# A second table in rank order, stored by SP, its row places carried by the first table; ranks computed ahead

## The chip, the cores and the metric

The kernel runs on one core of a Trainium2 chip. The metric is device time in microseconds (us), the median of several executions. Engines are named as in the profile: PE (TensorE, matmul), PEld (its weight load), DVE (VectorE), ACT (ScalarE), POOL (GpSimd), SP (SyncE, which here only issues DMAs).

## The reference, cut to what matters

A graph network of two layers over 6250 nodes and 100000 edges (sorted by destination), 16 node types, 32 edge types, 8 heads of 16 features, then a linear layer and a norm:

```python
k, q, v = (typed_linear(x, ntype, W).reshape(n, H, HS) for W in (Wk, Wq, Wv))
kT = jnp.einsum('nhd,htdo->nhto', k, Watt)      # for each node and edge type
vT = jnp.einsum('nhd,htdo->nhto', v, Wmsg)
kw = kT[src, :, etype]
m  = vT[src, :, etype]
a  = jnp.einsum('ehd,ehd->eh', kw, q[dst]) * pri[:, etype].T / SQRT_D
att = edge_softmax(a, dst, n)
hag = jax.ops.segment_sum((m * att[:, :, None]).reshape(-1, H * HS), dst, num_segments=n)
h = jax.nn.silu(typed_linear(hag, ntype, Wa))
# h is mixed with x by a gate of the node type, normalised, and is the next layer's x
```

After two layers: `x = layernorm(x + (h @ ff_w + ff_b))`.

## The kernel before, in words

**Tables.** For each layer the kernel writes a table into DRAM: a row for each node and edge type, 256 floats (128 of kT, 128 of vT). A tile `st` holds 128 nodes by 16 edge types by 256, 2 MB; a block of 128 nodes makes two of them (TG = 2). `table_block` (L287) fills one by eight groups of matmuls (L299) that ACT copies out of PSUM (L306), or DVE where `share` says so (L304); then `store` issues its DMA. An edge reads one row, number `src * 32 + etype`, kept in `ell`.

**Preparation and first table (L311 to L1030).** Nodes are sorted by type for the typed linear layers (`place`, `inv`, L371 to L431). `degrees` (L513) counts the edges of each destination: 64 passes over all edges on DVE (L537), four to a group, and for each group one-hot rows (L548 to L557) whose matmuls (L531) add the counts to the nodes. `rank_order` (L644) turns degrees and node types into a rank for each node, so that a block of 128 nodes has nearly equal degrees; rank is complete at L807. Its second half (L808 to L864) brings start, degree and type of each node into rank order, and then POOL gathers edge lists (`ell`, L869) and features (`xr`, L881) by rank. All of this is a generator (`ranking`) that the loop over first-table blocks (L1014 to L1030) advances a step at a time, so ranking and first table run side by side. The first table's rows are stored by `put0` (L1001): an indirect DMA of POOL, as nodes are in order of type there. `fetch` (L943) gathers x blocks for it with POOL.

**Layers (arm, L1034; edges, L1103).** For each of 50 blocks of 128 destinations, POOL gathers one table row per partition and edge slot (L1274), 867 gathers a layer, into `kvr`, a ring of 50 slots. DVE multiplies the rows with q (L1286), reduces (L1290), and `finished` (L1154) does softmax and weighted sums, a step at a time between the chunks of the next block. Three or four blocks make a superblock, of which there are 15. When one is complete, `nodes` (L1357) does its typed linear layer, gate and norm; in layer 0 it also computes k, v and q of the next layer, and `pieces_of` (L1478) the second table, with three `st` buffers. These generators are advanced by `tick` (L1116) in proportion to the slots gathered. `scatter` (L1483) stores an `st` tile by an indirect DMA of POOL, by the nodes' old numbers (`row2`), three half-steps after it is made. Layer 1's first gather waits for all of these stores.

**Order.** POOL's instructions stand as written (a manual schedule), so a scatter that waits for ACT's copies holds up the gathers behind it. The other engines' lists, SP's too, are ordered by the compiler's scheduler. SP loads `hr` (L1074), `ntb` (L1066) and q, and stores `hrd` (L1401) and `qrd` (L1452).

Of the kernel before, what the change touches and what calls it, by code (L numbers as in the profile page):

```python
# [18 lines left out]
P = 128  # L19
# [100 lines left out]
def kernel(  # L120
# [59 lines left out]

    tabs = [dram.tile([NP * RT, 2 * D], F32, name=f"tab{l}") for l in range(L)]
    kvs = dram.tile([PAD, 1], I32, name="kvs")
    typed = dram.tile([NB, P], BF16, name="typed")
# [102 lines left out]

    def table_block(pool, ps_pool, kT, vT, i, share, bufs, store, w=1):  # L287


        for tg in range(TG):  # L290
            tt = slice(tg * 16, (tg + 1) * 16)
            st = pool.tile([P, 16, 2 * D], F32, name="st", bufs=bufs)
            for half, (yT, bd) in enumerate(((kT, bdk), (vT, bdv))):
# [219 lines left out]
    def degrees(got):  # L513
# [10 lines left out]
        yield  # L524
        near = pp.tile([P, NEAR], F32, name="near")
        same = pp.tile([P, EC], BF16, name="same_dst", tag="eti")
        deg_ps = pps.tile([P, 2, NT], F32, name="ps")

        def products(c0, ol, oh):
            for c in range(c0, c0 + SB):  # L530
                nc.tensor.matmul(deg_ps, ol[:, c - c0, :], oh[:, c - c0],  # L531
                                 start=(c == 0), stop=(c == NEAR - 1))

        ready = None
        for c0 in range(0, NEAR, SB):
            for c in range(c0, c0 + SB):
                nc.vector.tensor_scalar(same, rel, float(c), None, op0=ALU.is_equal, op1=ALU.add,  # L537
                                        accum_out=near[:, c:c + 1])
                if c % 2:
                    yield "degrees"  # L540
            sl = slice(c0, c0 + SB)
            neari = pp2.tile([P, SB], I32, name="neari")
            nc.vector.tensor_copy(neari, near[:, sl])
            nears = pp2.tile([P, 2, SB], I32, name="nears")
# [97 lines left out]
    with tc.manual_schedule(engines={mybir.EngineType.Pool}):  # L642

        def rank_order():  # L644
# [161 lines left out]
            nc.vector.scalar_tensor_tensor(rank, rank, fits, nodef, op0=ALU.mult, op1=ALU.add)  # L806
            nc.vector.tensor_tensor(rank, rank, none, op=ALU.add)  # L807
            ranki = pp.tile([P, NT], I32, name="ranki")  # L808
            nc.vector.tensor_copy(ranki, rank)
# [188 lines left out]

        tables0 = []

        def put0(st, tg, b):  # L1001
            put = nc.gpsimd.indirect_dma_start(  # L1002
                out=tabs[0].rearrange("(n t) c -> n (t c)", t=16),
                out_offset=bass.IndirectOffsetOnAxis(ap=rows1[:, tg, b:b + 1], axis=0),
                in_=st.rearrange("p t c -> p (t c)"), in_offset=None,
                bounds_check=NP * TG - 1, oob_is_err=False)
            for other in tables0:
                tc.declare_no_dep(put.ins, other.ins, reason="rows of other nodes")
            tables0.append(put)

        got, stage = [], ""
        for _ in linears0(got, 0):
            pass
        for t in range(TY):  # L1014
            b0, _, b1 = spans(t)
            beside = linears0(got, t + 1) if t + 1 < TY else iter(())
            for b in range(b0, b1):
                def store(tg, st, b=b):
                    put0(st, tg, b)
                    fetch(min(b + AHEAD, fetched[0] + 1))  # L1020
                share = (1,) if stage in ("gathers", "done") else ()
                for half, _ in enumerate(table_block(tp, tnb, *got[t], b - b0, share, STB0, store)):
                    next(beside, None)
                    for _ in range(2 if half % 2 and stage is None else
                                   1 if half % 2 or stage != "gathers" else 0):
                        stage = next(ranking, "done")
# [7 lines left out]
    def arm(fast):  # L1034
# [9 lines left out]
        if fast:  # L1044
            kvr = npl.tile([P, SLOTS, 2 * D], F32, name="kv")
        eps = npl.tile([P, 1], F32, name="eps")
# [56 lines left out]
        def edges(l):  # L1103
# [50 lines left out]
            def finished(s, i, chunks, kvt, used, a, pair, sums, den):  # L1154
# [26 lines left out]
                for j in range(len(chunks) + 1):  # L1181
                    more = []
                    if j < len(chunks):
                        j0, j1 = chunks[j]
                        v = kvt[j][:, :, D:]
                        parts = [(0, j1 - j0)] if j else [
# [42 lines left out]
            for s, (i0, k, types) in enumerate(sbs):  # L1229
# [6 lines left out]
                for i in range(k):  # L1236
# [24 lines left out]
                    for j0, j1 in chunks:  # L1261
# [10 lines left out]
                        for j in range(j0, j1):  # L1272
                            at = KO[b] + j
                            get = nc.gpsimd.indirect_dma_start(  # L1274
                                out=kv[:, j - j0, :], out_offset=None, in_=tabs[l][:],
                                in_offset=bass.IndirectOffsetOnAxis(ap=ell[:, at:at + 1], axis=0))
                            if l == 1:
# [8 lines left out]
                        nc.vector.tensor_tensor(  # L1286
                            kk, kk, q.unsqueeze(1).to_broadcast([P, c, D]), op=ALU.mult)
                        for r in range(c):
                            if r == c // 3:
# [188 lines left out]
        def pieces_of(i0, k, kT, vT, share):  # L1478
# [4 lines left out]
            def scatter(tg, st, b):  # L1483
                put = nc.gpsimd.indirect_dma_start(  # L1484
                    out=tabs[1].rearrange("(n t) c -> n (t c)", t=16),
                    out_offset=bass.IndirectOffsetOnAxis(ap=row2[:, tg, b:b + 1], axis=0),
                    in_=st.rearrange("p t c -> p (t c)"), in_offset=None,
                    bounds_check=NP * TG - 1, oob_is_err=False)


                if fast:
                    for other in puts:
                        tc.declare_no_dep(put.ins, other.ins, reason="rows of other nodes")
                    puts.append(put)

# [189 lines left out]
```

## Time and profile before

| | |
|---|---|
| median of 3 runs | 3683.2 us (3673.7 to 3688.7) |
| profiled execution | 3703.7 us |
| its span, first to last instruction | 3701.5 us |
| busy: PE, DVE, ACT, POOL | 1811.8, 1953.0, 1018.8, 2150.0 us |
| first store of the first table starts | 61.1 us |
| rank complete (L807) | 266 us |
| first and last gather of layer 0 | 656.2 and 2221.3 us |
| first and last gather of layer 1 | 2306.4 and 3635.0 us |
| DMA | 691 MB, mean 187 GB/s |

The profile is of one execution. A row of a group gives its busy time, the mean duration of one instruction, and the idle time of its engine just before these instructions with what ended most of it ("issue" is time in which the engine waited for nothing that the profile shows; "remote" is a releaser that it can't name). A row of stretches gives, for a window of the span, the busy time of each engine with its number of instructions, the granted PE clock as a share of full speed, the mean busy share of 16 DMA engines, and GB/s. A row of waits gives the total, the number and the longest.

### The profile page before, as it was taken

How to read it: one execution, taken by the hardware profiler on the slowest of the kernel's cores; microseconds unless marked ns; L12 is line 12 of the kernel's file. 1: busy time of each engine (PE TensorE's matmuls, PEld its weight loads, DVE VectorE, ACT ScalarE, POOL GpSimd, SP SyncE). 2: the span in 40 equal slices, each digit the busy share in tenths (PEclk: the TensorE clock that was granted, in tenths of full speed). 3: DMA queues.
4: the chain of work that ended last, by engine and by line, in shares of the span. 5: the costliest groups of instructions: out<-in, count | busy, mean ns of one | idle time of the engine just before them, and what ended most of it. 6: DMA issues, size and time to landing. Idle time of an engine off the chain costs nothing. (4 is left out here: it accounts for less than half of the span.)

```text
span 3701.5 us, 22085 instructions
## 1 busy us (share of the span) xinstructions
PE 1811.8 (49%) x5612; PEld 822.8 (22%) x5612; DVE 1953.0 (53%) x4025; ACT 1018.8 (28%) x1677; POOL 2150.0 (58%) x2213
## 2 busy tenths in 40 slices
PE   3898998115555687658677675002120122112112
PEld 1344445002222232222222222001010111101011
DVE  8665231356355665457456633445655447455645
ACT  2675565002331244213332353001100111011111
POOL 2224663674676566666665652765667566666653
PEclk9789675557666776667678677555555555555555
DMA  6797999634655477546764677333333333333321
GB/s 181 309 385 319 399 403 403 161 99 147 218 188 195 140 269 268 176 148 210 268 220 165 241 284 304 107 96 91 95 92 107 86 89 102 92 99 94 91 82 43
DMA packets 194484, 691.11 MB, mean 187 GB/s; under 512 B 55469, under 2 KB 106032, under 8 KB 169298
## 3 DMA queue, kind: packets, MB, share of 16 engines
q0 software_dynamic: 119120, 651.15, 49.7%
q1 hardware_dynamic: 58838, 31.29, 3.2%
q10 hardware_dynamic: 16384, 7.11, 0.9%
q8 instruction: 48, 0.79, 0.1%
q14 instruction: 94, 0.77, 0.1%
HBM read 264.91 MB, written 429.48 MB: 188 GB/s over the span
## 5 line engine op out<-in xcount | busy, mean ns | idle before, releaser
L1274 POOL DMA_INDIRECT kv<-tab,ell x1734 | 1722.7, 993 | 769.2 <-issue 481.5
L306 ACT COPY st<-tb 128x512 f32<-128x512 f32 (+1 forms) x1064 | 726.1, 756 | 510.5 <-PE tb L299 255.0
L284 PE MATMUL nb<-ident,hag 128*128 128x128 f32 x100 | 26.1, 400 | 743.9 <-issue 212.5
L299 PE MATMUL tb<-bdv,kvT 32*128 32x512 f32 x800 | 275.7, 834 | 77.2 <-ACT st L306 66.2
L1484 POOL DMA_INDIRECT tab<-st,row x100 | 106.5, 1065 | 345.3 <-ACT st L306 288.5
L299 PE MATMUL tb<-bdv,vT 32*128 32x512 f32 x784 | 291.9, 868 | 24.4 <-ACT st L306 14.2
L299 PE MATMUL tb<-bdk,kvT 32*128 32x512 f32 x800 | 267.7, 824 | 67.5 <-ACT st L306 60.6
L1286 DVE TENSOR_TENSOR kv<-kv,q 128x896 f32<-128x896 f32 (+4 forms) x135 | 136.3, 1011 | 288.8 <-DMA kv<-tab,ell 260.4
L1290 DVE TENSOR_REDUCE a<-kv 128x48 f32<-128x768 f32 (+4 forms) x269 | 269.8, 1004 | 32.7 <-remote 23.2
L278 PE MATMUL nb<-xm,wa 128*128 128x384 f32 (+1 forms) x384 | 228.9, 758 | 117.5 <-DVE xm L269 79.3
L269 DVE SCALAR_TENSOR_TENSOR xm<-ntb,nb 128x384 f32<-128x384 bf16 (+1 forms) x336 | 184.4, 592 | 169.3 <-PE nb L284 50.6
L299 PE MATMUL tb<-bdk,kT 32*128 32x512 f32 x784 | 257.2, 865 | 0.9 <-issue 0.8
L1002 POOL DMA_INDIRECT tab<-st,rows x98 | 103.7, 1058 | 240.2 <-ACT st L306 195.1
L1286 DVE TENSOR_TENSOR kv<-kv,tb 128x768 f32<-128x768 f32 (+4 forms) x134 | 135.2, 1010 | 157.7 <-DMA kv<-tab,ell 130.7
L284 PE MATMUL nb<-ident,hs 128*128 128x128 f32 x100 | 37.8, 460 | 367.1 <-DVE hs L1395 165.1
L304 DVE COPY st<-tb 128x512 f32<-128x512 f32 (+1 forms) x120 | 89.1, 744 | 199.8 <-PE tb L299 141.1
L284 PEld LDWEIGHTS nb<-ident,hag 128*128 128x128 f32 x100 | 15.9, 198 | 762.5 <-issue 726.1
L278 PE MATMUL nb<-xm,wq 128*128 128x384 f32 (+1 forms) x192 | 106.7, 721 | 118.3 <-DVE m L1165 80.9
L1417 PE MATMUL nb<-xm,wkqv 128*128 128x384 f32 (+1 forms) x288 | 133.3, 617 | 51.0 <-DVE xm L269 32.6
L1200 DVE TENSOR_TENSOR tb<-kv,tb 128x512 f32<-128x512 f32 (+3 forms) x211 | 121.2, 574 | 69.5 <-remote 46.7
L278 PEld LDWEIGHTS nb<-xm,wa 128*128 128x128 f32 x384 | 98.7, 274 | 244.3 <-issue 113.4
L1436 PE MATMUL nb<-xm,wkqv 128*128 128x384 f32 (+1 forms) x288 | 132.3, 619 | 11.6 <-DVE xm L269 9.8
(314 smaller groups left out, 2745.4 us busy)
## 6 DMA issues: line engine op xcount, KB each, us to landing
kv<-tab,ell POOLq DMA_INDIRECT x1734
hr<-xrd SPq DMA_DIRECT2D x30, 192.0 KB
hr<-xrd SPq DMA_DIRECT2D x15, 256.0 KB
xrd<-xr POOLq DMA_DIRECT2D x11, 256.0 KB
ntb<-typed SPq DMA_DIRECT2D x20, 96.0 KB
hrd<-hs SPq DMA_DIRECT2D x10, 192.0 KB
qrd<-q SPq DMA_DIRECT2D x10, 192.0 KB
q<-qrd SPq DMA_DIRECT2D x10, 192.0 KB
```

Of the source, the lines that this page charges most:

```text
L269: nc.vector.scalar_tensor_tensor(xm[:, :n], ntb[:, :n], float(t), hT[:, :n], op0=ALU.is_equal, op1=ALU.mult)
L278: nc.tensor.matmul(ps[:, :n], w[:, t, :], xm[:, :n], start=(t == types[0]), stop=(t == types[-1]))
L299: nc.tensor.matmul(pt[:, b], yT[s, i * P:(i + 1) * P], bd[s, tt, :], start=True, stop=True)
L306: nc.scalar.copy(to, pt)
L1002: put = nc.gpsimd.indirect_dma_start(out=tabs[0].rearrange("(n t) c -> n (t c)", t=16), out_offset=bass.IndirectOffsetOnAxis(ap=rows1[:, t ...
L1200: nc.vector.tensor_tensor(acc[:, :n], v, acc[:, :n], op=ALU.add)
L1274: get = nc.gpsimd.indirect_dma_start(out=kv[:, j - j0, :], out_offset=None, in_=tabs[l][:], in_offset=bass.IndirectOffsetOnAxis(ap=ell[:, ...
L1286: nc.vector.tensor_tensor(kk, kk, q.unsqueeze(1).to_broadcast([P, c, D]), op=ALU.mult)
L1290: nc.vector.tensor_reduce(a[:, j0:j1, :], kk.rearrange("p k (h d) -> p k h d", h=H), axis=AX.X, op=ALU.add)
L1417: nc.tensor.matmul(outs[j][:, :n], wkqv[:, j, t, :], xm[:, :n], start=(t == types[0]), stop=(t == types[-1]))
L1436: nc.tensor.matmul(ps[:, :n], wkqv[:, j, t, :], xm[:, :n], start=(t == types[0]), stop=(t == types[-1]))
L1484: put = nc.gpsimd.indirect_dma_start(out=tabs[1].rearrange("(n t) c -> n (t c)", t=16), out_offset=bass.IndirectOffsetOnAxis(ap=row2[:, tg ...
```

## The change

1. The second table (`tab1`) is in order of rank: layer 1 reads row `rank(src) * 32 + etype`. Its blocks are then whole stretches of DRAM (rows of 16 KB, 32 KB apart), and SP stores them by a plain DMA in place of POOL's scatter.
2. To tell each edge its source's rank, the first table (`tab0`) gets a 257th column: `rank * 32 + edge type`. Layer 0's gathers bring it in, and DVE writes it over `ell`, which layer 1 reads. The ring's slots and the `st` tiles of the first table are 257 wide.
3. That column must be there when the first table is stored. So the loop over first-table blocks first runs `ranking` up to the rank, ranks go to DRAM through a transpose and a DMA by SP, and POOL gathers them in the order of types (`ask`, 49 gathers of 128 x 1). DVE adds the column in `put0`.
4. Half of the degree counts, those of destinations 32 to 63 of a partition's stretch, are no longer DVE passes: ACT sums the signs of (destination - c + 0.5) for 33 values of c, and DVE halves differences of neighbours. Groups of both kinds alternate.

```diff
+    W0 = 2 * D + 1
+    tab0 = dram.tile([NP * RT, W0], F32, name="tab_first")
+    tab1 = dram.tile([NR * RT, 2 * D], F32, name="tab_second")
+    ranks = dram.tile([NP, 1], F32, name="ranks")
...
+        HALF = NEAR // 2
+        near = pp.tile([P, HALF], F32, name="near")
+        edge = pp.tile([P, HALF + 1], F32, name="edge")
+        nc.vector.tensor_scalar(edge, colf[:, HALF:NEAR + 1], -1.0, 0.5, op0=ALU.mult, op1=ALU.add)
...
+        def signs_from(c):
+            nc.scalar.activation(sign, rel, AF.Sign, bias=edge[:, c:c + 1],
+                                 accum_out=signs[:, c:c + 1])
+
         ready = None
-        for c0 in range(0, NEAR, SB):
-            for c in range(c0, c0 + SB):
-                nc.vector.tensor_scalar(same, rel, float(c), None, op0=ALU.is_equal, op1=ALU.add,
-                                        accum_out=near[:, c:c + 1])
+        signs_from(0)
+        groups = range(0, NEAR, SB)
+        for c0 in [c for pair in zip(groups[:HALF // SB], groups[HALF // SB:]) for c in pair]:
...
+            if c0 < HALF:
+                for c in range(c0, c0 + SB):
+                    nc.vector.tensor_scalar(same, rel, float(c), None, op0=ALU.is_equal,
+                                            op1=ALU.add, accum_out=near[:, c:c + 1])
+                    signs_from(c + 1)
...
+            else:
+                at0 = c0 - HALF
+                diff = pp2.tile([P, SB], F32, name="diff")
+                nc.vector.tensor_tensor(diff, signs[:, at0:at0 + SB], signs[:, at0 + 1:at0 + SB + 1],
+                                        op=ALU.subtract)
+                nc.vector.tensor_scalar(neari, diff, 0.5, None, op0=ALU.mult)
...
             nc.vector.tensor_tensor(rank, rank, none, op=ALU.add)
+            scaled = pp.tile([P, NT], F32, name="scaled")
+            nc.vector.tensor_scalar(scaled, rank, float(RT), None, op0=ALU.mult)
+            rk_ps = pps.tile([NT, P], F32, name="ps")
+            nc.tensor.transpose(rk_ps, scaled, ident)
+            rkr = pp.tile([NT, P], F32, name="rkr")
+            nc.vector.tensor_copy(rkr, rk_ps)
+            nc.sync.dma_start(ranks.rearrange("(i p) c -> i (p c)", p=P), rkr)
+            yield "ranked"
...
+        def ask(end):
+
+            while asked[0] < min(end, NT):
+                g = asked[0]
+                nc.gpsimd.indirect_dma_start(
+                    out=ranked[:, g:g + 1], out_offset=None, in_=ranks[:],
+                    in_offset=bass.IndirectOffsetOnAxis(ap=inv[:, g:g + 1], axis=0))
+                asked[0] += 1
 
         def put0(st, tg, b):
+            nc.vector.tensor_scalar(st[:, :, 2 * D], colf[:, tg * 16:(tg + 1) * 16],
+                                    ranked[:, b:b + 1], None, op0=ALU.add)
             put = nc.gpsimd.indirect_dma_start(
-                out=tabs[0].rearrange("(n t) c -> n (t c)", t=16),
+                out=tab0.rearrange("(n t) c -> n (t c)", t=16),
...
+        while stage != "ranked":
+            stage = next(ranking)
+        ask(4)
         for t in range(TY):
...
                     put0(st, tg, b)
+                    if tg:
+                        ask(asked[0] + 1)
...
-            kvr = npl.tile([P, SLOTS, 2 * D], F32, name="kv")
+            kvr = npl.tile([P, SLOTS, W0], F32, name="kv")
...
-                                out=kv[:, j - j0, :], out_offset=None, in_=tabs[l][:],
-                                in_offset=bass.IndirectOffsetOnAxis(ap=ell[:, at:at + 1], axis=0))
+                                out=kv[:, j - j0, :2 * D if l else W0], out_offset=None,
+                                in_=(tab1 if l else tab0)[:], in_offset=bass.IndirectOffsetOnAxis(ap=ell[:, at:at + 1], axis=0))
...
+                        if l == 0:
+                            nc.vector.tensor_copy(ell[:, KO[b] + j0:KO[b] + j1], kv[:, :, 2 * D])
...
             def scatter(tg, st, b):
-                put = nc.gpsimd.indirect_dma_start(
+                if fast:
+                    puts.append(nc.sync.dma_start(
+                        tab1.rearrange("(n g t) c -> g n (t c)", g=TG, t=16)[
+                            tg, b * P:(b + 1) * P, :], st.rearrange("p t c -> p (t c)")))
+                    return
+                nc.gpsimd.indirect_dma_start(
```

More of the change, by code (lines that the diff above doesn't have):

```diff
@@ L285, in transposed, with table_block @@
         return tr
-    def table_block(pool, ps_pool, kT, vT, i, share, bufs, store, w=1):
+    def table_block(pool, ps_pool, kT, vT, i, share, bufs, store, w=1, cols=2 * D):
         for tg in range(TG):
             tt = slice(tg * 16, (tg + 1) * 16)
-            st = pool.tile([P, 16, 2 * D], F32, name="st", bufs=bufs)
+            st = pool.tile([P, 16, cols], F32, name="st", bufs=bufs)
             for half, (yT, bd) in enumerate(((kT, bdk), (vT, bdv))):
@@ L524, in degrees @@
         yield
-        near = pp.tile([P, NEAR], F32, name="near")
+        HALF = NEAR // 2
+        near = pp.tile([P, HALF], F32, name="near")
+        edge = pp.tile([P, HALF + 1], F32, name="edge")
+        nc.vector.tensor_scalar(edge, colf[:, HALF:NEAR + 1], -1.0, 0.5, op0=ALU.mult, op1=ALU.add)
+        signs = pp.tile([P, HALF + 1], F32, name="signs")
+        sign = pp.tile([P, EC], BF16, name="sign", tag="onehot")
         same = pp.tile([P, EC], BF16, name="same_dst", tag="eti")
@@ L532, in products @@
                                  start=(c == 0), stop=(c == NEAR - 1))
+        def signs_from(c):
+            nc.scalar.activation(sign, rel, AF.Sign, bias=edge[:, c:c + 1],
+                                 accum_out=signs[:, c:c + 1])
         ready = None
-        for c0 in range(0, NEAR, SB):
-            for c in range(c0, c0 + SB):
-                nc.vector.tensor_scalar(same, rel, float(c), None, op0=ALU.is_equal, op1=ALU.add,
-                                        accum_out=near[:, c:c + 1])
-                if c % 2:
-                    yield "degrees"
+        signs_from(0)
+        groups = range(0, NEAR, SB)
+        for c0 in [c for pair in zip(groups[:HALF // SB], groups[HALF // SB:]) for c in pair]:
             sl = slice(c0, c0 + SB)
             neari = pp2.tile([P, SB], I32, name="neari")
-            nc.vector.tensor_copy(neari, near[:, sl])
+            if c0 < HALF:
[3 more added lines that the diff above has]
+                    signs_from(c + 1)
+                    if c % 2:
+                        yield "degrees"
+                nc.vector.tensor_copy(neari, near[:, sl])
+            else:
[4 more added lines that the diff above has]
+                nc.vector.tensor_scalar(neari, diff, 0.5, None, op0=ALU.mult)
             nears = pp2.tile([P, 2, SB], I32, name="nears")
@@ L999 @@
         tables0 = []
+        ranked = pp.tile([P, NT], F32, name="ranked")
+        asked = [0]
+        def ask(end):
[5 more added lines that the diff above has]
+                asked[0] += 1
         def put0(st, tg, b):
+            nc.vector.tensor_scalar(st[:, :, 2 * D], colf[:, tg * 16:(tg + 1) * 16],
+                                    ranked[:, b:b + 1], None, op0=ALU.add)
             put = nc.gpsimd.indirect_dma_start(
-                out=tabs[0].rearrange("(n t) c -> n (t c)", t=16),
+                out=tab0.rearrange("(n t) c -> n (t c)", t=16),
                 out_offset=bass.IndirectOffsetOnAxis(ap=rows1[:, tg, b:b + 1], axis=0),
@@ L1019, in store @@
                     put0(st, tg, b)
+                    if tg:
+                        ask(asked[0] + 1)
                     fetch(min(b + AHEAD, fetched[0] + 1))
                 share = (1,) if stage in ("gathers", "done") else ()
-                for half, _ in enumerate(table_block(tp, tnb, *got[t], b - b0, share, STB0, store)):
+                for half, _ in enumerate(table_block(tp, tnb, *got[t], b - b0, share, STB0, store,
+                                                         cols=W0)):
                     next(beside, None)
@@ L1184, in finished @@
                         j0, j1 = chunks[j]
-                        v = kvt[j][:, :, D:]
+                        v = kvt[j][:, :, D:2 * D]
                         parts = [(0, j1 - j0)] if j else [
@@ L1488, in scatter @@
                     bounds_check=NP * TG - 1, oob_is_err=False)
[L1491 to L1494, printed above, removed]
             def steps(gen):
```

## The prediction, made before the changed kernel ran

> **What bounds the kernel now.** I read the page first: POOL is the busiest engine (58% of the span) and one line of it, the gather of table rows, has most of its time. Then I cut the trace into stretches at the first and last gather of each layer, asked for POOL's lines and waits in each, then for DVE's waits. From the page (busy us, mean ns of one | idle time before them, and what ended it):
>
> ```profile
> L1274 POOL DMA_INDIRECT kv<-tab,ell x1734 | 1722.7, 993 | 769.2 <-issue 481.5
> ...
> L1484 POOL DMA_INDIRECT tab<-st,row x100 | 106.5, 1065 | 345.3 <-ACT st L306 288.5
> ...
> L1002 POOL DMA_INDIRECT tab<-st,rows x98 | 103.7, 1058 | 240.2 <-ACT st L306 195.1
> ```
>
> The stretches (PE, PEld, DVE, ACT, POOL busy, PE clock, DMA share, GB/s): ranking beside the first table, the rest of that table, gathers of layer 0, its tail, gathers of layer 1:
>
> ```profile
> 44.00:266.00 222.00, 185.93 (x871) 87.85 (x872) 159.01 (x440) 142.56 (x282) 67.58 (x76) 0.77 0.77 314
> 266.00:656.00 390.00, 342.88 (x1186) 177.74 (x1184) 129.50 (x265) 222.24 (x429) 199.12 (x211) 0.71 0.94 380
> 656.00:2222.00 1566.00, 960.80 (x2664) 383.47 (x2664) 852.53 (x1586) 466.35 (x621) 993.25 (x955) 0.68 0.58 199
> 2222.00:2306.00 84.00, 53.99 (x198) 21.33 (x196) 31.74 (x56) 34.39 (x46) 12.51 (x13) 0.77 0.80 325
> 2306.00:3636.00 1330.00, 240.60 (x586) 133.98 (x586) 716.67 (x1498) 135.03 (x272) 864.38 (x907) 0.53 0.33 95
> ```
>
> Both layers issue 867 gathers; layer 0 needs 1566 us for them, layer 1 1330. POOL's lines in layer 0, then in layer 1:
>
> ```profile
> L1274 POOL DMA_INDIRECT kv<-tab,ell x867 | 899.3, 1037 | 306.6 <-issue 240.3 <-DVE acc L1189 18.3 <-DMA tab<-st,rows 17.2
> L1484 POOL DMA_INDIRECT tab<-st,row x88 | 94.2, 1070 | 283.1 <-ACT st L306 251.1 <-issue 18.0 <-ACT a L1170 5.6
> ```
>
> ```profile
> L1274 POOL DMA_INDIRECT kv<-tab,ell x867 | 823.4, 950 | 462.6 <-issue 241.3 <-DVE v L1334 61.8 <-DVE tb L1189 44.8
> L1517 POOL DMA_INDIRECT out_dram<-o,node x40 | 41.0, 1024 | 12.2 <-issue 12.2
> ```
>
> An undisturbed gather takes 0.95 us with 0.30 us to the next (the timeline shows this gap before nearly every one, told as issue). In layer 0 POOL spends 94.2 us on 88 scatters of the second table and 283.1 us idle ahead of them, because a scatter waits for ACT's copies while gathers stand behind it. In layer 1 there is no scatter of that kind, but POOL waits 462.6 - 241.3 = 221 us for DVE to release slots of the 50-slot ring. That second wait is what I expect to see more of.
>
> **Part 1, scatter leaves POOL (layer 0).** Removed from POOL's stretch: 94.2 + 283.1 = 377 us. What is late next? POOL alone needs 867 x (1.037 + 0.30) = 1159 us; I keep the 1.037, since nothing says that the extra 87 ns come from the scatters. DVE alone: its waits in layer 0 (total, times, longest) are
>
> ```profile
> DVE kv L1286 <- DMA kv<-tab,ell: 252.6, 52, 12.6
> DVE xm L269 <- remote: 84.3, 20, 10.0
> ...
> DVE kv L1286 <- issue: 28.2, 8, 6.5
> ...
> DVE hs L1384 <- remote: 20.0, 3, 8.2
> ```
>
> Busy 852.5, idle 713.5, of which 280.8 for gathered rows; so with rows always there DVE's own stream lasts 1566 - 281 = 1285 us. The change adds 135 copies of row places (L1339 of the new kernel); the nearest rows, small casts of L543, take 0.16 to 0.17 us: 23 us, 1308 in all. Its waits ended by "remote" (84 + 20) stand behind PE and ACT, which wait for table buffers; a store issued as soon as the copy is done should return about half, say 50: 1260. How do two such streams run together? Layer 1 shows it: POOL alone 823.4 + 41.0 + 907 x 0.30 = 1137, DVE alone 1330 - 157 (waits for rows) = 1173, together 1330, so 157 above the longer one. For layer 0 I take 1260 + 130 = 1390 (less than 157, as POOL has more slack there). Bounds: 1205 (all remote waits gone) + 60 = 1265, and 1308 + 157 = 1465. Gain 1566 - 1390 = **176 us** (101 to 301).
>
> The transfers: table stores stay 2 MB each, on SP's queue instead of POOL's. DMA share 0.58 of 1566 is 908 us of work, 65% of 1390: not the bound. SP's issue of a store costs some 0.36 us (hr and q rows); 100 of them are 36 us on an engine that is idle. The tail of 84 us stays, as it is the last blocks' PE and ACT work; as POOL ends further ahead of the others, I add 10 us.
>
> A rule against this part: the Trainium skill, "DMA: Bandwidth & Descriptors", section "Issuing engines are not separate DMA queues", says that all issuers share the same 16 DMA engines and that spreading saves only the issuing time. By it alone the gain would be 88 x 1.37 = 121 us. The row shows 283 us more of waiting in POOL's order, which the rule does not speak of.
>
> **Part 2, rows of 257 elements.** No row of the trace has such a pitch; the nearest, POOL's gathers of 4-byte to 1 KB rows (L869, L881, L1274), all take 0.95 to 1.04 us, so issue is unchanged. If a row cost as much transfer as two, the 0.52 us of DMA time per gather (0.33 x 1330 / 867 = 0.51) would double: 908 + 440 = 1348 of 1390, just the bound; below, nothing is gained. I take nothing, as 1028 bytes are 0.4% more than 1024. Nor is a loss sure to be excluded at DVE, whose reads of such rows get a new pitch; its rows (L1286, L1290, 1.0 us each) would show it.
>
> The same page, section "How a descriptor splits into AXI transactions", says a read that starts off a 256-byte boundary fetches from the boundary below. An estimate by it: 128 bytes more on average, 13% of 0.51 us, hidden under POOL's 1.34. No row here has unaligned starts.
>
> **Part 3, ranks ahead (first table).** Before, the first store starts at 61.1, the ranks are ready at 266, 98 stores end at
>
> ```profile
> 638.02 0.98 POOL L1002 DMA_INDIRECT tab<-st,rows  x1 [4.51 <-ACT st L306]
> 656.19 1.00 POOL L1274 DMA_INDIRECT kv<-tab,ell  x1 [17.19 <-DMA tab<-st,rows]
> ```
>
> Now no store starts before the ranks are out. DVE's chain from 44.5: 32 passes of L537 x 1.04 (0.963 + 0.082) = 33; 16 groups (one-hots, two products, small casts) x 2.2 (121.7 to 123.8 in the timeline) = 35; 8 x 0.3 for differences of signs, and copies of hT, kT, vT: 4; to 117. Degree, prefix and key took 172.2 to 179.1: 7; 13 key blocks 10 (21 before, with waits for a PE full of table work); the chain to L766 14.4, of which PE waits shrink: 11; 13 blocks of L791 to L797 at 3.3 = 43; last eight operations 1: 189. Transpose, copy, SP's store of the ranks and its landing some 5 (the chain of L858 to L863, without a landing in the trace; 2 to 10); then POOL issues four rank gathers and four x gathers, 8 x 1.25 = 10, before the first store: **205 us**, 144 later. ACT's 33 sign passes: 128x512 copies take 0.50 to 0.61 us, so 782 elements about 0.9 us, 30 us beside 32 copies (16 us) in a window of 65: hidden, up to 1.4 us each. If that cover were gone, each 0.1 us more costs 3 us.
>
> Then 98 stores. Before, from 377.8 to 638.0, 48 intervals took 5.4 us each (DMA share 0.99 to 1.00 in those slices); from 269 to 313, beside the second part of the ranking, 7.6 to 9.9. POOL now issues per store 1.32, half a rank gather, half an x gather, two ell or xr gathers: 1.32 + 0.62 + 0.62 + 2.5 = 5.1 us, nearly level with that; so for the 57 stores with all of these I take 5.5, for six beside the ranking 8, for 34 others 5.4: 48 + 314 + 184 = 546, last store 751, landed 769 (18 as before) against 656. I take **+110**; with 5.3 throughout and ranks 10 sooner it is 727, +71; with 5.9 for the 57, 5.5 for the 34 and ranks 10 later 804, +148.
>
> **Sum** against the profiled execution (3703.7, span 3701.5): +110 - 176 + 10 = -56. Layer 1 is unchanged. Median shown: 3683.2, 20 below the profiled one; the same -56 gives **3627**.
>
> **Rivals.** (a) POOL's floor: DVE's waits were mostly caused by the scatter, layer 0 takes 1265: 110 - 301 + 10 = -181, 3502. For it: 251 us of ACT waits in POOL. Against: layer 1, without scatters, is 157 above its longer stream. (b) The ring takes the scatter's place: DVE's remote waits stay (1308) and ring and latency add 140, nearly layer 1's 157: 1448, gain 118, +2: 3685, no change. For it: the 221 us of layer 1, with less DVE work there. Against: remote waits that a store in time would end. (c) Slower, by SP's order. A store now stands in SP's queue behind loads that wait for others:
>
> ```profile
> SPq L1074 <- ACT hb L1374: 456.1, 11, 119.9
> ```
>
> If stores are late there, buffers come free late, ACT and PE stall as now, and layer 0 keeps 1510 to 1566: +64 to +120, 3775 in the middle. It decides once layer 0 takes over 1566 - 120 = 1446. Against: in the compiled list most such loads stand where their releaser comes early, and three buffers give room. (d) The store or the long rows do not do what they should: strided 16 KB rows or unaligned gathers make DMA the bound, which the doubled gathers' 1348 plus layer 1's 157 would do: 1505, +59, 3742.
>
> **How the numbers follow.** Forecast (layer 0 at 1330 to 1428, so 3567 to 3665): 0.45; (a) 0.13; (b) 0.17; (c) 0.21; (d) 0.04. Half a per cent, 18 us, is about what a measurement of this kernel tells from no change: faster 0.58, same 0.17, slower 0.25. The range takes in (a) with a first table 30 us better (+80 in place of +110), and all of (c) but its upper half: 3470 to 3770.
>
> **What would show it.** First store near 205 and first layer-0 gather near 769; no ACT wait among POOL's in layer 0, but 150 to 300 us of waits for DVE; layer 0's gathers in 1390 us at a DMA share near 0.65; layer 1 within 10 us of 1330. I am wrong if the first gather of layer 0 comes after 805, if DVE waits for rows as long as before (transfer or SP's order), or if gathers take over 1.1 us.

## The result and the profile after

The changed kernel takes 3897.3 us (median, 3895.5 to 3909.6) beside 3685.0 us for the kernel before: ratio 1.0589, 95% interval 1.0557 to 1.0621. It is slower by 5.9%. The forecast was 3627, and its range ended at 3770.

The page of the changed kernel (busy us, mean ns of one | idle time before them, and what ended it):

```profile
L1324 POOL DMA_INDIRECT kv<-tab_first,ell x867 | 947.3, 1093 | 589.6 <-issue 236.9
L1324 POOL DMA_INDIRECT kv<-tab_second,ell x867 | 823.2, 949 | 669.4 <-issue 239.0
L1046 POOL DMA_INDIRECT tab_first<-st,rows x98 | 99.4, 1014 | 199.6 <-ACT st L310 173.5
L1339 DVE CAST ell<-kv 128x7 int32<-128x7 f32 (+4 forms) x135 | 24.9, 185 | 334.8 <-DMA kv<-tab_first,ell 303.8
```

The scatter's line is gone, and so are POOL's waits for ScalarE in layer 0. Yet POOL is idle ahead of layer 0's gathers for 590 us, of which 237 are the usual short gaps. New is the last line: 135 copies of row places are busy for 25 us, and DVE stands idle for 335 us ahead of them, 304 of that for gathered rows.

The same cut into stretches as before (PE, PEld, DVE, ACT, POOL busy, PE clock, DMA share, GB/s): ranking, first table, gathers of layer 0, its tail, layer 1:

```profile
44.00:175.00 131.00, 68.07 (x364) 39.17 (x365) 117.59 (x373) 48.66 (x100) 11.23 (x13) 0.57 0.03 8
175.00:759.00 584.00, 539.92 (x1692) 258.21 (x1692) 194.44 (x436) 321.63 (x608) 298.27 (x323) 0.71 0.92 373
759.00:2284.00 1525.00, 767.24 (x2184) 314.91 (x2184) 795.60 (x1609) 371.22 (x502) 947.33 (x867) 0.67 0.55 180
2284.00:2501.00 217.00, 180.66 (x676) 70.81 (x676) 83.44 (x168) 129.87 (x164) 0.00 (x0) 0.84 0.80 322
2501.00:3830.00 1329.00, 239.35 (x586) 132.79 (x586) 717.56 (x1500) 136.24 (x273) 864.37 (x908) 0.53 0.33 95
```

Against the stretches of before: the first gather comes 103 us later, layer 0's gathers take 41 us less, the tail 133 us more, layer 1 is level. 103 - 41 + 133 = 195; the two profiled executions differ by 192 (3895.8 and 3703.7). Against the forecast's terms (+110, -176, +10) the loss lies in the gathers, 135 us, and in the tail, 123 us. The gathers' stretch has too little gain, and the tail is two and a half times as long. In it 676 matmuls and 164 ScalarE instructions are left over; before there were 198 and 46.

DVE's waits in layer 0's gathers (in all, times, longest), then POOL's:

```profile
DVE ell L1339 <- DMA kv<-tab_first,ell: 296.0, 46, 11.8
DVE kv L1336 <- DMA kv<-tab_first,ell: 100.7, 21, 10.4
DVE kv L1336 <- issue: 46.0, 12, 7.3
...
DVE ell L1339 <- issue: 31.0, 7, 7.4
```

```profile
POOL kv L1324 <- DVE acc L1239: 134.9, 10, 42.5
POOL kv L1324 <- DVE kv L1239: 87.8, 7, 34.9
```

DVE waits for POOL's rows, and POOL waits for DVE to free slots: DVE 474 us in its four lines (281 in the two of before), POOL 223 us in its two. Neither stream alone sets the pace; some order makes them wait for each other.

The place to look is the compiled list of DVE, which its scheduler puts in order (in this kernel POOL alone keeps the order in which the program is written). A stretch of it, cut to the operations:

```
L1250 acc<-kv,acc
L1339 ell<-kv
L1255 sums<-acc
L1339 ell<-kv      x2
L273  xm<-ntb,nb   x16
L1336 kv<-kv,q
```

The three copies are those of chunks 73 to 75; the last line is the product of chunk 68 (the trace shows 7.2 and 6.8 us of idle time ahead of the second and third copy). A copy reads column 256 of a row, which no other instruction writes, so it may stand anywhere behind the gathers of its rows. The product of the same rows (L1336) must also wait for the query. Counted over the trace, 60 of the 135 copies stand ahead of their own product, up to nine chunks ahead, while the ring holds 50 rows, some eight chunks.

### The profile page after: what moved, and what is told of

The parts are those of the page before. It is cut to its first block, busy times and chain, and to the rows that moved or that the text cites. A ratio compares the mean times of both kernels' runs of the same rounds, so it can differ in the third digit from the quotient of the medians.

```text
span 3893.6 us, 22369 instructions
## 1 busy us (share of the span) xinstructions
PE 1822.9 (47%) x5613; PEld 834.3 (21%) x5613; DVE 1972.1 (51%) x4273; ACT 1024.6 (26%) x1675; POOL 2134.2 (55%) x2162
## 5 line engine op out<-in xcount | busy, mean ns | idle before, releaser
L1324 POOL DMA_INDIRECT kv<-tab_first,ell x867 | 947.3, 1093 | 589.6 <-issue 236.9
L1324 POOL DMA_INDIRECT kv<-tab_second,ell x867 | 823.2, 949 | 669.4 <-issue 239.0
L303 PE MATMUL tb<-bdv,vT 32*128 32x512 f32 x784 | 330.1, 870 | 11.6 <-ACT st L310 7.2
L303 PE MATMUL tb<-bdk,kT 32*128 32x512 f32 x784 | 323.2, 876 | 11.2 <-DVE st L308 6.6
L303 PE MATMUL tb<-bdv,kvT 32*128 32x512 f32 x800 | 242.2, 811 | 71.0 <-ACT st L310 43.6
L308 DVE COPY st<-tb 128x512 f32<-128x512 f32 (+1 forms) x188 | 135.4, 722 | 240.3 <-PE tb L303 188.5
L1336 DVE TENSOR_TENSOR kv<-kv,q 128x896 f32<-128x896 f32 (+4 forms) x135 | 134.9, 1008 | 190.8 <-DMA kv<-tab_first,ell 100.7
L1336 DVE TENSOR_TENSOR kv<-kv,tb 128x768 f32<-128x768 f32 (+4 forms) x134 | 135.3, 1011 | 156.9 <-DMA kv<-tab_second,ell 131.3
L1046 POOL DMA_INDIRECT tab_first<-st,rows x98 | 99.4, 1014 | 199.6 <-ACT st L310 173.5
L1339 DVE CAST ell<-kv 128x7 int32<-128x7 f32 (+4 forms) x135 | 24.9, 185 | 334.8 <-DMA kv<-tab_first,ell 303.8
L1250 DVE TENSOR_TENSOR tb<-kv,tb 128x512 f32<-128x512 f32 (+3 forms) x211 | 121.0, 573 | 73.5 <-remote 50.3
L1469 PE MATMUL nb<-xm,wkqv 128*128 128x384 f32 (+1 forms) x288 | 125.8, 588 | 63.3 <-DVE xm L273 37.3
L303 PEld LDWEIGHTS tb<-bdk,kT 32*128 32x128 f32 x784 | 123.0, 245 | 118.7 <-ACT st L310 39.3
```

The source lines that it names most:

```text
L303: nc.tensor.matmul(pt[:, b], yT[s, i * P:(i + 1) * P], bd[s, tt, :], start=True, stop=True)
L308: nc.vector.tensor_copy(to, pt)
L1046: put = nc.gpsimd.indirect_dma_start(out=tab0.rearrange("(n t) c -> n (t c)", t=16), out_offset=bass.IndirectOffsetOnAxis(ap=rows1[:, tg, ...
L1250: nc.vector.tensor_tensor(acc[:, :n], v, acc[:, :n], op=ALU.add)
L1324: get = nc.gpsimd.indirect_dma_start(out=kv[:, j - j0, :2 * D if l else W0], out_offset=None, in_=(tab1 if l else tab0)[:], in_offset=bass ...
L1336: nc.vector.tensor_tensor(kk, kk, q.unsqueeze(1).to_broadcast([P, c, D]), op=ALU.mult)
```

## The experiments

In these runs the kernel before takes 3336 to 3350 us, not 3685. The traces show one difference. In the first comparison DVE's waits that end with no event seen ("remote") sum to 386 us in the kernel before; in every trace of the experiments they sum to nothing, and layer 1 takes 1149 us in place of 1330. So all comparisons below stay within the experiments, with the kernel before timed beside each; the first question is whether the loss is there too.

All in one table (us from the traces; ratio of the medians to the kernel before, 95% interval):

| kernel | first gather | gathers, layer 0 | tail | ratio |
|---|---|---|---|---|
| before (b1) | 657 | 1393 | 85 | 1 |
| changed (a1) | 728 | 1416 | 217 | 1.0688 (1.0670 to 1.0706) |
| e1 without copies | 729 | 1257 | 175 | 1.0080 (1.0049 to 1.0111) |
| e2 POOL's plain store | 729 | 1364 | 85 | 1.0175 (1.0151 to 1.0199) |
| e3 scatter back, no copies | 728 | 1395 | 85 | 1.0247 (1.0224 to 1.0270) |
| e4 before, SP's store only | 657 | 1252 | 180 | 0.9857 (0.9838 to 0.9877) |
| e5 copies behind the sums | 729 | 1245 | 174 | 1.0056 (1.0034 to 1.0078) |
| e6 e5, POOL's plain store | 728 | 1354 | 84 | 1.0120 (1.0103 to 1.0137) |
| e7 e5, pieces at 0.6 | 729 | 1277 | 203 | 1.0209 (1.0191 to 1.0226) |
| e8 e5, counts on DVE | 760 | 1244 | 172 | 1.014 (one run) |
| e9 e5, ScalarE's queue | 729 | 1415 | 186 | 1.0587 (1.0565 to 1.0609) |
| e10 before, late 7 | 657 | 1376 | 107 | 1.0037 (1.0020 to 1.0053) |
| e13 changed, DVE in written order | 730 | 1215 | 104 | 0.9701 (0.9685 to 0.9717) |
| e14 before, DVE in written order | 647 | 1395 | 91 | 0.9971 (0.9957 to 0.9985) |
| e15 changed, all in written order | 730 | 1258 | 113 | 0.9842 (0.9823 to 0.9861) |
| e16 e13, ScalarE's queue | 730 | 1217 | 125 | 0.9761 (0.9744 to 0.9778) |

Layer 1 is 1143 to 1150 in all of them.

**The two kernels again.** No edit.

> The changed kernel as it is, beside the kernel with the copies of places behind the sums (1.006 of the kernel before, where layer 0's gathers took 1244 us and the tail 175). Theory P (copies of places far ahead in DVE's list): the gathers of layer 0 are over 80 us longer than there, by waits for rows and for slots, ratio 1.03 to 1.06. Theory S (the chip of the first comparison stalls by itself: there DVE's waits that end with no event seen by the profile sum to 386 us in the kernel before, and in the four runs of the first experiments to nothing): if this run has none of them, the copies cost only their 25 us, ratio 1.00 to 1.015.

> The kernel before as it is, for its stages on this chip. If DVE has none of the waits without an event, POOL's gathers of layer 1 follow each other without waits for slots (867 x 1.327 = 1150 us, as in the four runs), layer 0 takes about 1390 and its tail about 85: 3336 in all. If the waits are there, 3685 as in the first comparison.

Measured: theory P for the changed kernel, with 1.0688 by even more than it said, and no "remote" wait in it; 3344.9 for the kernel before. So those waits did not make the loss. Here the stages before and after are (gathers of layer 0, tail; first the kernel before):

```profile
656.70:2050.00 1393.30, 911.90 (x2664) 373.75 (x2664) 852.31 (x1586) 464.75 (x620) 1002.21 (x956) 0.71 0.66 224
2050.00:2135.00 85.00, 57.90 (x200) 22.93 (x196) 31.76 (x56) 34.88 (x47) 12.17 (x12) 0.71 0.79 321
```

```profile
728.00:2144.00 1416.00, 735.06 (x2184) 308.69 (x2184) 792.96 (x1609) 368.39 (x502) 935.63 (x867) 0.69 0.59 194
2144.00:2361.00 217.00, 183.25 (x676) 71.33 (x676) 83.47 (x168) 129.68 (x164) 0.00 (x0) 0.83 0.80 322
```

The change costs 71 us ahead of the first gather, 23 in the gathers and 132 in the tail: 226, and the spans differ by 224.

**The copies left out (e1) or put behind the sums (e5).**

```diff
-                        if l == 0:
-                            nc.vector.tensor_copy(ell[:, KO[b] + j0:KO[b] + j1], kv[:, :, 2 * D])
...
                                 nc.vector.tensor_reduce(
                                     a[:, j0:j1, :], kk.rearrange("p k (h d) -> p k h d", h=H),
                                     axis=AX.X, op=ALU.add)
+                                if l == 0:
+                                    nc.vector.scalar_tensor_tensor(
+                                        ell[:, KO[b] + j0:KO[b] + j1], a[:, j0:j1, 0], 0.0,
+                                        kv[:, :, 2 * D], op0=ALU.mult, op1=ALU.add)
```

e1 has the first part alone, so its layer 1 reads rows of other nodes; e5 has both.

> The changed kernel without the 135 copies of row places on DVE; layer 1 then gathers by the first table's places, so it reads rows of other nodes (that part of the computation is left out). Theory P (places): the compiled list of DVE puts a copy wherever its rows are modelled as landed, up to eight chunks ahead of the product of its own rows, so DVE stands waiting for rows while the work that frees ring slots is queued behind it, and POOL waits for the slots. Then without the copies the gathers of layer 0 fall from 1525 to about 1390 us, DVE's waits for rows from 474 to under 300, POOL's waits for DVE from 353 to under 200, the tail from 217 to 84 to 130: 3640 to 3740 us in all. Theory O (order): with the store out of POOL's written order, table work is put off and the loads on SP's queue wait behind stores; then nothing changes but the copies' own 25 us: gathers at least 1490, tail about 200, 3850 to 3900. Theory R (rows of 1028 bytes cost the gathers and the DMA): as O, 3870 to 3900.

> The changed kernel complete, with each copy of places written as zero times the chunk's first head sum plus the place, so that it can stand in DVE's list only after the sum of its own rows. Theory P: nearly all of the loss by the copies goes: gathers 1390 to 1430, tail 84 to 130, 3650 to 3760, within 25 us of the kernel without copies. Theory O: 3860 to 3910, as the changed kernel. Theory R: 3870 to 3910.

Measured: gathers 1257 and 1245 against 1416, so P is right on the gathers, and by more than it said. e5 does all of the changed kernel's work with as many copies, and is 6% faster than it; the copies' work is not the cost, their place in the list is. Little else moved between a1 and e1: beside the copies, 98% of DVE's instructions and 99% of ScalarE's stand in the same order. DVE's waits for rows and POOL's for slots, changed kernel (a1), then e5:

```profile
DVE ell L1339 <- DMA kv<-tab_first,ell: 328.5, 49, 15.6
DVE kv L1336 <- DMA kv<-tab_first,ell: 164.8, 39, 10.5
...
POOL kv L1324 <- DVE acc L1239: 96.1, 9, 29.0
POOL kv L1324 <- DVE kv L1239: 78.2, 10, 35.3
```

```profile
DVE kv L1336 <- DMA kv<-tab_first,ell: 235.6, 55, 10.8
...
POOL kv L1324 <- DVE acc L1239: 12.0, 3, 6.0
...
POOL kv L1324 <- DVE kv L1239: 7.8, 11, 4.8
```

DVE's 493 us become 236, POOL's 174 become 20. But P said of the tail 84 to 130, and it is 174 to 175: that part of P fell. Something else makes the tail.

**One half of the change each (e3, e4).** e3 is e1 with the scatter of before:

```diff
-                                in_=(tab1 if l else tab0)[:], in_offset=bass.IndirectOffsetOnAxis(ap=ell[:, at:at + 1], axis=0))
+                                in_=(tabs[1] if l else tab0)[:], in_offset=bass.IndirectOffsetOnAxis(ap=ell[:, at:at + 1], axis=0))
...
-                if fast:
-                    puts.append(nc.sync.dma_start(
...
+                put = nc.gpsimd.indirect_dma_start(
```

e4 is the kernel before with SP's store, and layer 1 gathering from its table by the first table's places, so rows of other nodes:

```diff
             def scatter(tg, st, b):
+                if fast:
+                    puts.append(nc.sync.dma_start(
+                        tab1.rearrange("(n g t) c -> g n (t c)", g=TG, t=16)[
+                            tg, b * P:(b + 1) * P, :], st.rearrange("p t c -> p (t c)")))
+                    return
```

> The changed kernel with the second table's store put back to POOL's scatter by node, and without the copies of places: what is left of the change is the rows of 257, the ranks ahead and the signs. Theories P and O: only the later start of about 103 us remains, gathers 1566 and tail 84 as before: 3780 to 3800. Theory R: the gathers of layer 0 lengthen too, to at least 1620: 3840 to 3900.

> The kernel before with only the second table's store moved to SP's queue and to rank order; rows of 256, no ranks ahead, no copies; layer 1 gathers by the first table's places, so it reads rows of other nodes. Theory P: the gain of the prediction shows alone: gathers of layer 0 at 1390, tail 84 to 100, 3510 to 3540. Theory O: gathers 1500 or more and a tail of 200: 3730 to 3800. Theory R: 3500 to 3540, as P.

Measured: e3 has the gathers and the tail of before (1395, 85) and starts 71 us later: rows of 257 elements cost the gathers nothing, theory R falls. (In e3 scatters hold POOL up and could hide a cost; without them, e1 with rows of 257 takes 1257 and e4 with rows of 256 takes 1252, a gather 1.103 and 1.101 us on average.) e4 shows the moved store alone: gathers 141 us shorter, as P had it, and a tail 95 us longer, as O had it. Of the 100 stores, 12 were issued after the last gather in the kernel before, 28 in e4, 27 in e5. In e4 and e5 they come 6.1 us apart on average, at a DMA share of 0.87: the tail is work that was not done beside the gathers.

**Who issues the store (e2, e6, e9).** e2 is the changed kernel, e6 is e5, with `nc.gpsimd.dma_start` in place of `nc.sync.dma_start`; e9 is e5 with `nc.scalar.dma_start`.

> The changed kernel with its plain copies of places, whose only edit is that POOL issues the second table's stores at their written place between its gathers. In this kernel's list of DVE 7 of the 135 copies stand ahead of the product of their own rows, in the changed kernel's 60, up to nine chunks ahead. Theory P: the copies cost their own 25 us and no more, so this is within 15 us of the kernel with ordered copies and POOL's store (gathers 1354, tail 84, ratio 1.012). Rival C (the copies themselves, or their writes to the list of places, cost 200 us wherever they stand): gathers over 1500, ratio 1.06 to 1.08.

> The kernel with the places behind the sums, its second store issued by POOL at its written place between the gathers, to rank order, in place of SP. Theory O (POOL's order paces the gathers to the table work, and the tail is the table work that gathers have run away from): gathers about 1390 and tail about 85 again, as with the scatter; the sum of both, 1479 there and 1419 with SP's store, is near 1479; ratio 1.02 to 1.03. Rival: the transfer itself makes the tail (a store of strided rows is slower than a scatter): tail 175 whichever queue issues it.

> The kernel with the places behind the sums, its second store issued on ScalarE's queue in place of SP's, so that no load stands behind a store that waits. Theory Q (SP's order, the prediction's rival c: SP waited over 700 us ahead of stores, and loads of rows, types and queries stood behind): gathers and tail together fall by 20 us or more from 1419, ratio under 1.0. Rival (those loads are early enough; gathers and tail are set by POOL's rate and then by the store transfers): within 12 us of 1419, ratio 1.003 to 1.01.

Measured: e6 has a tail of 84 with the same transfer of strided rows, so the transfer is not what makes the tail. Its sum (1438) is below the 1479 expected by 41 us; POOL issues a plain store in 0.58 us and a scatter in 1.04, which makes 41 us for the 89 stores among the gathers. e2 keeps the plain copies and is 5 per mille above e6: copies that stand in their place cost next to nothing (7 of 135 stand ahead in its list). So the copies' loss comes only together with the moved store: with stores in POOL's written order the list has the copies in their places, without them it has not.

e9 missed both expectations: gathers 1415. No load stands behind its stores, and it is slower: freeing SP's order (rival c of the prediction) gains nothing. Its waits are those of the changed kernel again, without a copy in the way (DVE 411 us for rows at L1336, POOL 172 us for DVE's L1239). In its list of DVE the products themselves stand further ahead: on average 9.0 chunks past the last summed block (at 2.7 chunks a block), against 7.9 in e5 and in the changed kernel, and 6.8 before. That made a new theory, L: the scheduler orders DVE by its own reckoning of when rows land; without stores in POOL's written order it reckons them earlier, and puts row work further ahead and table work further back.

**Table work earlier in the program (e7), scatters later (e10).**

```diff
-  (1.0 if s + 4 < len(sbs) else 0.6) * slots(min(s + 2, len(sbs) - 1))
+  0.6 * slots(min(s + 2, len(sbs) - 1))
```

```diff
-                    late.append([3, (tg, st, b)])
+                    late.append([7, (tg, st, b)])
```

> The kernel with the places behind the sums, with the pieces of every superblock's second table spread over 0.6 of the slots in place of 1.0, as the last four superblocks have them already. Theory O: the tail is put-off table work, so table work earlier in the lists shortens it by 20 to 60 us while the gathers lengthen by less: ratio 0.985 to 1.0. Rival (TensorE, DVE and the transfers have no room earlier, since DVE stands waiting for rows 300 us of the gathers and TensorE waits for DVE): tail and gathers together stay within 10 us of 1419, ratio 1.005.

> The kernel before with each scatter of the second table written seven steps behind its copies in place of three, so one table later in POOL's order. If POOL's waits for the copies (121 us from the first gather to layer 1's start) are what the scatter costs, they fall by half or more and layer 0 and its tail by 40 to 80 us: ratio 0.975 to 0.99. Rival (the table buffers, three of them, come free later, so copies wait for scatters in their turn): ratio 0.995 to 1.02.

Measured: e7 missed both, gathers 32 and tail 29 us longer than e5. Its list has 126 DVE instructions between the last product of layer 0 and the first of layer 1, e5's 92: written earlier, table work came later on DVE. e10 gained 17 in the gathers and lost 22 in the tail: later scatters gain next to nothing.

**The counts back on DVE (e8).** e5 with the 64 passes of before at L537 to L566.

> The kernel with the places behind the sums and all 64 degree counts on DVE again, as before the change. By the prediction's row (1.04 us a pass) the 32 further passes put the first store 33 us later less the 8 differences of signs, at about 205 in place of 175; the first table's end, which the transfers set, and the gathers shift by 20 to 33 us, the whole by as much: ratio 1.011 to 1.016. Rival: the chain to the ranks waits for something else, first store under 185.

Measured: first store at 205.7 in place of 175.2, first gather 31 us later, the rest level. The signs earn what their row said; a sign pass takes 0.95 us and the read of its sum 0.20 on ScalarE, hidden.

**DVE in written order (e13, e14, e15, e16).** One edit, on the changed kernel (e13) and on the kernel before (e14):

```diff
-            ctx2.enter_context(tc.manual_schedule(engines={mybir.EngineType.Pool}))
+            ctx2.enter_context(tc.manual_schedule(engines={mybir.EngineType.Pool, mybir.EngineType.DVE}))
```

e16 is e13 with the store on ScalarE's queue; e15 names PE, ACT and SP as well.

> The changed kernel with its plain copies and SP's store, whose only edit is that DVE too keeps the order in which the program writes its instructions, as POOL does. No copy then stands ahead of its product, and 61 DVE instructions stand between the last product of layer 0 and the first of layer 1 (changed kernel 96, before 56). Theory L (DVE's compiled list is the cause of both losses): gathers at most 1300 and tail at most 140, in all 0.97 to 1.005 of the kernel before. Rival (a written order knows nothing of waits and stalls DVE more): gathers over 1400, ratio over 1.03.

> The kernel before with DVE in written order, the control. Theory L: POOL's scatters set the pace, so within 1 per cent of the kernel before. Rival: over 1.03, as for the changed kernel.

> The changed kernel with DVE in written order and the second store on ScalarE's queue. Theory L: the queue alone matters little, within 20 us of the same kernel with SP's queue (without the written order ScalarE's queue cost 180 us, gathers 1414). Rival (a store on ScalarE's queue holds ScalarE up): 60 us or more above it.

> The changed kernel with all engines in written order. If the lists of TensorE, ScalarE and SP have no part, within 20 us of the kernel with DVE alone in written order; if put-off table work in their lists makes the tail, 40 us or more below it. The other way (they stall in order): above it by more than 20.

Measured: as theory L forecast. Gathers and tail of e13, then of e14:

```profile
729.70:1944.70 1215.00, 836.31 (x2580) 349.60 (x2582) 855.26 (x1706) 449.35 (x602) 920.35 (x867) 0.76 0.74 254
1944.70:2049.20 104.50, 76.10 (x285) 31.44 (x280) 40.69 (x72) 49.34 (x65) 0.48 (x2) 0.79 0.84 342
```

```profile
647.30:2041.90 1394.60, 888.26 (x2605) 370.99 (x2606) 853.89 (x1582) 456.22 (x608) 1012.40 (x955) 0.73 0.65 223
2041.90:2133.00 91.10, 64.27 (x257) 25.89 (x255) 35.39 (x61) 43.65 (x58) 12.37 (x12) 0.84 0.75 304
```

With DVE's order held, the change comes near its forecast: first gather 82 us later, gathers 180 us shorter, tail 13 us longer, and 3252.6 us against 3341.1. The order alone is worth 0.3% to the kernel before (e14) and 9% to the changed one (0.9701 and 1.0688); with it in both kernels the change gains 2.6%. In e13 DVE waits 175 us for rows, and POOL 10 us for DVE's `acc` of L1239. e16 is 18 us above e13, where e9 was 178 above e5: the queue itself costs little, and what it did in e9 came with the list. e15 is 47 us above e13, so the scheduler's lists of the other engines are better than the written ones. e13 is the fastest version tried: 3.0% below the kernel before.

The edit of e13 does not move DVE's instructions alone: the scheduler answers it with a somewhat different order of ScalarE and SP too. Against a1, a third of DVE's instructions stand elsewhere, and a tenth of ScalarE's. But the order of DVE in e13, e15 and e16 is one and the same, the lists of ScalarE and SP differ between them, and all three keep most of the gain (gathers 1215 to 1258, tails 104 to 125).

What the gathers then wait for, POOL's lines show, of the kernel before (b1), e5 and e13:

```profile
L1274 POOL DMA_INDIRECT kv<-tab,ell x867 | 910.5, 1050 | 295.5 <-issue 223.3 <-DMA tab<-st,rows 17.6 <-DMA tab<-st,row 9.9
L1484 POOL DMA_INDIRECT tab<-st,row x89 | 92.5, 1040 | 113.2 <-ACT st L306 82.1 <-issue 17.1 <-DMA kv<-tab,ell 9.1
```

```profile
L1324 POOL DMA_INDIRECT kv<-tab_first,ell x867 | 948.0, 1093 | 309.0 <-issue 221.9 <-DMA kv<-tab_first,ell 14.1 <-DMA tab_first<-st,rows 12.3
```

```profile
L1324 POOL DMA_INDIRECT kv<-tab_first,ell x867 | 920.8, 1062 | 307.1 <-issue 215.4 <-DMA kv<-tab_first,ell 32.8 <-DMA tab_first<-st,rows 12.5
```

In e5 and e13 little but POOL itself sets the pace: 867 gathers of that duration, with the usual gap of 0.305 us, make 1212 us of the 1245 and 1185 of the 1215; e1 and e4 are as near (1221 of 1257, 1219 of 1252). So the written order finds in the gathers only 30 us that e5 does not have, and 27 of them are shorter gathers; its larger part over e5 is the tail, 70 us.

## Why the prediction was wrong

Point by point; the profiles of the first comparison decide, and the experiments say why:

- **Ranks ahead: right in the sum, by luck in part.** First gather forecast at 769, measured 759 (+103, forecast +110). But the first store came at 175, not 205 (the chain to the ranks was quicker), and from there to the first gather it took 584 us, not 564. In the experiments, where that stretch takes 553, the shift is +71, the lower bound.
- **Rows of 257: right**, nothing: the gathers' stretch takes 1395 us with them (e3) and 1393 without. The Trainium skill, "DMA: Bandwidth & Descriptors", section "How a descriptor splits into AXI transactions", has a read that starts off a 256-byte boundary fetch more; what that may add does not show here. That no row of the kernel before has unaligned starts was misread: L869 gathers 4-byte entries from wherever a node's edges begin, in 0.96 us like the others.
- **Sign passes hidden: right** (e8).
- **The copies: the step that failed most.** The prediction added them to DVE's stream at 23 us, by the duration of small casts. Their busy time is 25. What it left out is where they stand: 60 of 135 ahead of their own products, waiting for rows with everything else of DVE behind them. a1 against e5: 1416 - 1245 = 171 in the gathers and 217 - 174 = 43 in the tail, 214 us for 25 us of work.
- **"The tail of 84 us stays", plus 10: failed.** By the moved store alone it grew by 95 (e4). The prediction took it to be the last blocks' work whatever happens ahead of it. POOL's scatters were a cost, and they were also the pace: POOL could not gather on while the table was behind. Without them gathers run ahead, and 27 to 31 of 100 stores are left over in place of 12 (e4, e5, a1). With DVE's order held 14 are left, and the tail grows by 13.
- **Layer 0's gathers at 1390, gain 176: failed.** The changed kernel gained 41, and in the experiments lost 23. The stream of DVE was taken to last as long as before, but its list was a different one. With the order held the gain is 180 (e14 to e13); that this is near 176 is luck, as the terms behind it were others. The sum had DVE as the longer stream (1260 us) and 130 us for two streams running together. In the experiments the same working gives DVE 1393 - 422 (waits for rows) = 971 us in the kernel before, layer 1 is 12 us above POOL's stream in place of 157, and POOL is the longer one (1175 us, 867 gathers with their gaps). The 377 us taken from POOL are 206 there (92.5 and 113.2 in b1's row of scatters). The 50 us of "remote" waits returned fit the first comparison, where these waits of DVE in the gathers went from 114 to 66 us; the experiments have none.
- **The rule against this part.** The gathers gain 141 us in e4 and 180 in e13, more than the 121 us that the prediction estimated for issuing alone by the Trainium skill, "DMA: Bandwidth & Descriptors", section "Issuing engines are not separate DMA queues". The waits in POOL's order came on top; but e4 gives 95 us back in the tail.
- **Rival (a), POOL's floor,** described the gathers once the copies were out of the way: 1245 to 1257 in e1, e4 and e5, 1215 in e13, where it had 1265. The tail it had wrong like the forecast.
- **Rival (b), the ring takes the scatter's place:** POOL did wait for slots, 174 us at L1239 in a1, but with the same ring 20 us in e5. The copies' place made the waits. **Rival (d):** neither the long rows (e1 beside e4) nor the strided store (e6) shows a cost.
- **Rival (c), slower by SP's order**, had the sign and not the cause. Its 3775 came from buffers freed late; SP does wait for ScalarE's copies (675 us ahead of stores in e5's gathers), but a queue without loads behind the stores does not help (e9, e16).
- **What would show it wrong** named "DVE waits for rows as long as before (transfer or SP's order)". DVE waited longer, for neither reason: the list of possible causes had no place for the order of DVE's own instructions.

Shown by runs: the copies' place (e1, e5, e2), the moved store's tail (e4, e6), and that one written order of DVE ends both losses and does nothing for the kernel before (e13 with e14; e15 and e16 with other lists beside it). Not separated: what part of the shorter tail is due to ScalarE's list, which changes with DVE's. Argued only: that the scheduler reckons rows to land earlier when no store stands in POOL's order; the lists show what it did, not why. How far ahead the products stand does not explain it alone: in the written list it is 7.4 chunks on average, more than the 6.8 of before.

## What to carry to other kernels

Price an added instruction twice: by its duration, and by where it lands in its engine's list, with all that is then behind it; an instruction that needs only a transfer and not the work beside it is free to go far ahead and stall everything. A wait that looks like pure loss may be the pace that keeps two streams together: before taking it away, ask what orders them afterwards. Where a scheduler orders an engine, compare its list before and after a change, and tie or write by hand the order that the pace relied on.

## What the runs showed of the hardware beside this

- POOL's gather instruction has a median of 0.946 to 0.949 us in both layers, but in the experiments' layer 0 a mean of 1.04 (e10) to 1.10 us (e1), single ones up to 8.2 us (e3); in layer 1, at a DMA share of 0.38, the mean is 0.95 and the longest 1.4. The 87 ns over the undisturbed row that the prediction could not place are there without any scatter too. The long ones fall together with DVE's products over the ring's rows (L1239, L1250, L1336): in e5's layer 0 the 469 gathers beside none of these take 0.956 us on average, the 77 that have them for nine tenths of their time or more 1.377. But in layer 1 the same products change nothing (0.949 and 0.946), so the cause stays open.
- POOL issues a plain store of 128 rows of 16 KB in 0.58 us (e6, 89 of them beside the gathers), the scatter of such rows in 1.04 (b1).
- The kernel before took 10% longer in the first comparison than in the experiments (3685 and 3345 us), level until the first gather (656 and 657 us), then with waits on DVE, TensorE and ScalarE (386, 138 and 300 us) that no event in the trace ends. POOL, DVE, ScalarE and SP run the same instructions in the same order in both. What these waits are stays open.
